# Block one keeps twenty tiles of its third convolution in place of sixteen and takes the statistics of twelve from a Gram matrix; the fused stage visits the tiles in a new order

## Chip, cores and metric

One core of one Trainium2 chip runs the whole program in one launch. The metric is the device time of that launch in microseconds (us). All data is float32. TensorE (PE) multiplies, VectorE (DVE), ScalarE (ACT) and GpSimd (POOL) do elementwise work, and DMAs are issued from the queues of SyncE (SP), ACT and POOL.

## The reference

Two residual bottleneck blocks run one after the other over 64 images of 1024 channels and 14x14 pixels. Batch norm uses the statistics of the whole batch, so each convolution must be known (or at least its mean and variance) for all images before any of its outputs can be scaled.

```python
def block(x, w1, b1, g1, be1, w2, b2, g2, be2, w3, b3, g3, be3, residual_scale):
    out = relu(_bn(_conv(x, w1, b1, 1, 0), g1, be1))      # 1x1, 1024 -> 256
    out = relu(_bn(_conv(out, w2, b2, 1, 1), g2, be2))    # 3x3, 256 -> 256
    out = _bn(_conv(out, w3, b3, 1, 0), g3, be3)          # 1x1, 256 -> 1024
    return relu(x + softplus(residual_scale)[0] * out)
x = block(x, ...)   # layer 0
x = block(x, ...)   # layer 1
```

## The kernel before

**Tiles and stages.** The batch is cut into T = 32 tiles of two images (392 pixels). A tile of x is 128 partitions by 8 rows (output-channel blocks `o`) by 392. The 256-channel output of conv 2 stays on chip for all tiles (`y_all`, 2 blocks). The stages are: conv 1 of block one; conv 2 of block one; `mixed`; `fused`; conv 2 of block two; `gram` of block two; `final`. The change touches `mixed` and `fused`.

**Seven products.** A 1x1 convolution of one unit is done as seven block products instead of eight (class `Seven`): `p1` to `p7`, with sums of the inputs made beforehand by elementwise engines. `Conv1` (block two's conv 1) has seven products of four matmuls each per tile, 28 in all; after `p1` it makes its input sums on DVE (`at3`, L439, then `at2`, L440, then `at1`, L441), `p6` needs `at2`, `p5` needs `at1`, and `p7`'s result is copied by ACT and added by DVE (L427). `Conv3` and `Direct` (conv 3) have seven products of one matmul each per unit, four units (`q`) per tile.

**Mixed.** Tiles are numbered so that 0 to KEPT-1 are the Gram tiles and KEPT to 31 the kept ones (KEPT = 16). Conv 3 of the kept tiles is computed here: tile KEPT whole in `first`, the other 15 as 60 `Direct` units. Their raw outputs z go to DRAM by DMA (`z<-kept`) and their statistics come from `bn_stats`. The Gram tiles' statistics come from the Gram matrix of their normed y: y is moved by DMA into `homes` (`move`, pieces `MOVES`), transposed by DVE (`turn`) in chunks of 128 pixels, and multiplied by `gram_products`, four small matmuls per chunk, in batches of BATCH = 4 chunks placed between units by the list `at`. 16 tiles are 6272 pixels, 49 chunks. `conv3_stats` turns the Gram matrix into mean and variance of conv 3 (no output of the Gram tiles is computed here), `bn_aggr` merges all entries (L1614), `affine` gives scale and shift. In the last units `bring` starts loading the first eight z rows (`at_first`).

**Fused.** The order of places is `positions()`: places 0, 2, 4 ... hold Gram tiles, places 1, 3, 5 ... kept ones. For each place x is loaded (`coming`, five buffers, the load for place p+4 at step 12 of place p, in four DMAs on SP), block one's third convolution is added, relu follows, the result is stored for block two's residual (`mid<-x`, ACT queue) and `Conv1` of block two reads it. For Gram places `last_convs` runs `Conv3` units: their matmuls are made here, DVE adds four parts (L514), POOL two, ACT does the relu. For kept places `kept_rows` takes the rows of z back from DRAM: an even row is one DVE operation (L1839), an odd row two POOL operations (L1825, L1826). A row's z lies in one of eight places in `y_all` that were loaded ahead (AHEAD = 8): the row eight further on is brought, by an SP DMA, when a row has been used (`behind`, `bring`). Only the last two tiles' rows use other places (28-element lines of `y_all`), and the last tile comes whole.

**The order.** One Python loop with a counter `k` writes the program, and each engine runs its part in that order. Step k gives one matmul of `Conv1` (28 steps per place). Beside it `done < LEAD + (k + 1) // 2` gives one `Conv3` matmul per two steps, and `k % 7 == 3` one kept row per seven steps. Before the loop, 14 `Conv3` matmuls (LAG) and seven rows are written. The rows of a step are written before its `Conv1` matmul, so they stand ahead of what that matmul's product asks of DVE.

Of the kernel before, what the change touches and what calls it, by code (L numbers as in the profile page):

```python
# [34 lines left out]

LAG, LEAD = 14, 10

KEPT = T // 2
NGRAM = KEPT * PX
MOVES = 5 * P * CH, 5 * P * CH, 5 * P * CH, 5 * P * CH, 9 * P  # L40
BATCH = 4
ROWS = 5 * CS, 13 * CS
AHEAD = 8


# [24 lines left out]
def bottlenecks(ctx: ExitStack, tc: tile.TileContext, x, w1s, w2s, w3s, pars, out):  # L70
# [1192 lines left out]
    def gram(psum, pool, homes, aff, minus_c, beside):  # L1263
# [142 lines left out]
                beside[k]()  # L1406
        return upper, lower, by, gs

    def positions():
        return [KEPT * (p % 2) + p // 2 for p in range(T)]  # L1410

    def beds(spare):


        places, before, last = [], {}, {}
        for r in range((T - KEPT - 1) * CS):
            t, o = KEPT + r // CS, r % CS
            if r < ROWS[1]:
                g, i = (NG - 3, NG - 1)[r >= ROWS[0]], r % AHEAD
                a = g * GPX + i % 4 * PX  # L1420
                key, v = (g, i), y_all[:, i // 4, a : a + PX]
            else:
                ring = [(u, s) for s in range(MS) for u in range(t, T)]
                i = o - MS
                key = ("spare", o % MS) if i < 0 or i >= len(ring) else ring[i]
                v = spare[key[1]] if key[0] == "spare" else two(*key)
            places.append(v)
            if key in last:
                before[r] = last[key]
# [15 lines left out]
    def mixed(psum, pool, one, x_right, x_left, aff, minus_c, w3, made_c, summed_c, summed_a, mv3, xs, coming_x):  # L1445
# [28 lines left out]

        def home(k):
            a, e = pieces[k]
            x = homes[k % 2][:, : MS * (e - a)].rearrange("p (s j f) -> p s j f", s=MS, j=4)
            return x, a, (e - a) // 4

        def quarter(k, i):  # L1480
            (a, e) = pieces[k]
            h = (e - a) // 4
            return slice(a + i * h, a + i * h + h)
# [8 lines left out]
        def move(k, i, places):  # L1492
            assert normed[k] >= MS * i + MS and (k < 2 or k - 2 in turned)
            for j in places:
                tc.keep_in_program_order(
                    nc.sync.dma_start(
                        out=home(k)[0][32 * i : 32 * i + 32, :, j], in_=y_all[32 * j : 32 * j + 32, :, quarter(k, i)]
                    )
                )
                moved[k] += 1  # L1500

        def blocks(t):
            return [[two(t, s)[:, i * H // 2 : (i + 1) * H // 2] for i in range(2)] for s in range(MS)]
# [63 lines left out]
        def chunks():  # L1567

            for k, (a, e) in enumerate(pieces):
                x, count = home(k)[0], (e - a) // P  # L1570
                for i in range(0, count, CH):
                    zt = next(zts)
                    turn(zt, x, i, min(CH, count - i))
                    if i + CH >= count:
                        assert moved[k] == 16
                        turned.add(k)
                    for c in range(min(CH, count - i)):
                        yield zt[:, c], (k, i + c)

        def batches():  # L1580
            queue, total = chunks(), NGRAM // P
            bounds = [*range(0, total, BATCH), total]
            ready = [[]]
            for _ in range(BATCH // CH):
                ready[0].extend(itertools.islice(queue, CH))
                yield
            for a, e in zip(bounds, bounds[1:]):
                for i, (v, _) in zip(range(a, e), ready.pop()):
                    gram_products(upper, lower, v, i == 0, i == total - 1, True)
                yield  # L1590
                ready.append([])
                for _ in range(BATCH // CH):
                    ready[0].extend(itertools.islice(queue, CH))
                    yield
# [2 lines left out]
        coming = {t: prepare(t) for t in range(KEPT + 1, T)}  # L1597
        tail, grams = None, iter(())
        moves = {}
        for k, begin in enumerate((3, 13, 20, 28), 1):  # L1600
            for i in range(8):
                moves[begin + i] = moves.get(begin + i, ()) + ((k, i // 2, (i % 2 * 2, i % 2 * 2 + 1)),)
        at = list(range(9, 48, 3))
        at_first, _ = beds((None, None))
        made = []

# [24 lines left out]
        for unit, step in stream:  # L1631
            t, q = KEPT + 1 + unit // 4, unit % 4
            if step == 1 and unit > 0:
                next(norms, None)
            if step == 3 and at[0] - 3 < unit < at[0]:
                grams = batches() if unit == at[0] - 2 else grams
                next(grams)
            if step == 2 and unit in at or step == 3 and (unit in at or unit - 1 in at):
                next(grams, None)
            if step == 3:  # L1640
                if q < 2 and t + 1 < T:
                    next(coming[t + 1], None)
                if 0 < unit <= 32 and unit % 2 == 0:
                    center((unit - 1) // 8 + 1, (unit - 1) % 8 // 2)
                for where in moves.get(unit, ()):
                    move(*where)
                if unit in (20, 23, 26, 29):
                    next(summed_a)
                if unit in (44, 48):
                    coming_x()  # L1650
                if 50 <= unit < 50 + AHEAD:
                    bring(at_first[unit - 50], unit - 50)
                if unit == 57:
                    assert next(tail, "end") == "end"
                    for half in range(2):
                        to = gram_entry[:, :, 3 * half : 3 * half + 3]
                        nc.gpsimd.memset(to[:, :, 0], NGRAM / 2)
                        run(nc.vector.tensor_copy(to[:, :, 1], mv3[:, :, 0]))
                        run(nc.vector.tensor_scalar(to[:, :, 2], mv3[:, :, 1], NGRAM / 2, None, ALU.mult))
            if step == 5 and q == 1 and t + 1 < T:  # L1660
                next(coming[t + 1], None)
            if step == 5 and unit == 57:
                column_sums(pool, blocks(positions()[2]), n, eng=nc.gpsimd, to=ahead())
            if unit == 59 and step in (3, 5):
                aggregated(step // 4)
            if step == 6 and unit > at[-1] + 1 and (tail is None or unit < 57):
                if tail is None:
                    assert next(grams, "end") == "end"
                    tail = conv3_stats(
                        psum, pool, (upper, lower, by, gs), w3, mv3, ("ax", "ap", "ax", "ap"), homes[1], ("ax", "ax", "ap")  # L1670
                    )
                next(tail, None)
# [116 lines left out]
    def fused(psum, pool, one, right, coming, xs, raw, w1, w3, aff, par, stats, border, begun):  # L1789
# [12 lines left out]
            behind[q].append(r)  # L1802

        def last_convs():
            for p in range(2, T, 2):
                t = places[p]
                ys = [[two(t, s)[:, i * H // 2 : (i + 1) * H // 2] for i in range(2)] for s in range(MS)]
                sums = column_sums(pool, ys, n, **(dict(to=ahead(), made=True) if p == 2 else {}))
                for q in range(CS // 2):
                    yield Conv3(psum, pool, xs[p], q, n, ys, sums, w3, aff, mids[t] if q == CS // 2 - 1 else None, one)  # L1810

# [4 lines left out]
        def kept_rows():  # L1816
# [10 lines left out]

            for o in 1, 3, 5:
                by_pool(*row(o, 1, o), o)
            for r, (p, o) in enumerate(itertools.product(range(1, T, 2), range(CS))):  # L1830
                while r == len(at) and later:
                    later.pop(0)()
                    yield
# [22 lines left out]

        whole = []
        pinned.append(True)
        a, c, rows = stream(first_convs(), T), stream(last_convs(), (KEPT - 1) * CS // 2), kept_rows()
        done, ended = LAG, None  # L1860
        for i in range(LAG):
            next(c)
            if i == 2:
# [4 lines left out]
        for k in itertools.count():  # L1868
# [7 lines left out]
                    nc.sync.dma_start(out=whole[0].rearrange("p s f -> p (s f)"), in_=zs[T - 1 - KEPT])  # L1876
                )
            late = k - 28 * (T - 4)
            if (late >= 30 and late % 5 == 0) if late >= 20 else k % 7 == 3:
                next(rows, None)  # L1880
            if next(a, "end") == "end":
                break
            while done < LEAD + (k + 1) // 2:
                if next(c, "end") == "end" and ended is None:
                    ended = k
                done += 1
            if ended is not None and k >= ended + 8:
                while waiting:
                    waiting.pop(0)()
        assert next(c, None) is None and next(rows, None) is None and not waiting  # L1890
# [322 lines left out]
```

## Time and profile before

| what | value |
|---|---|
| median of 3 runs | 1895.61 us (1895.54 to 1896.14) |
| profiled execution, its own time | 1896.71 us |
| span of its instructions | 1894.6 us |
| DVE, ACT, POOL busy in the span | 1574.0, 1092.0, 748.4 us |
| `mixed`, about | 586 to 787 us of the span |
| `fused`, about | 787 to 1235 us |
| mean DMA rate over the span | 242 GB/s |

Times inside the trace are microseconds from the span's start. A float32 matmul shows as two records, so counts of PE records are twice the matmuls of the program. A row of the timeline gives start, duration, engine, line, operation, output and input by name, and count of merged instructions; behind it, in brackets, stands how long the engine was idle before and what ended that. A few matmul records are missing from the trace.

### The profile page before, as it was taken

How to read it: one execution, taken by the hardware profiler on the slowest of the kernel's cores; microseconds unless marked ns; L12 is line 12 of the kernel's file. 1: busy time of each engine (PE TensorE's matmuls, PEld its weight loads, DVE VectorE, ACT ScalarE, POOL GpSimd, SP SyncE). 2: the span in 40 equal slices, each digit the busy share in tenths (PEclk: the TensorE clock that was granted, in tenths of full speed). 3: DMA queues.
4: the chain of work that ended last, by engine and by line, in shares of the span. 5: the costliest groups of instructions: out<-in, count | busy, mean ns of one | idle time of the engine just before them, and what ended most of it. 6: DMA issues, size and time to landing. Idle time of an engine off the chain costs nothing. (4 is left out here: it accounts for less than half of the span.)

```text
span 1894.6 us, 28577 instructions
## 1 busy us (share of the span) xinstructions
PE 1876.6 (99%) x9778; PEld 1563.6 (83%) x9778; DVE 1574.0 (83%) x2484; ACT 1092.0 (58%) x2275; POOL 748.4 (40%) x764
## 2 busy tenths in 40 slices
PE   9999999999999999999999999999999999999999
PEld 5555557999997998899999999999999986555555
DVE  5787867999998776778878788799999986888886
ACT  2222214677777665555555555457777692666666
POOL 0111100121206555377676776501121141666665
PEclk9999999999999999999999999999999999999999
DMA  7777654797764555678788889459788467799997
GB/s 288 271 252 258 223 184 131 206 217 219 206 201 161 181 177 204 248 272 308 279 278 309 281 302 285 193 168 223 212 208 226 141 160 289 262 346 345 334 354 270
DMA packets 262369, 458.19 MB, mean 242 GB/s; under 512 B 59152, under 2 KB 228976, under 8 KB 249040
## 3 DMA queue, kind: packets, MB, share of 16 engines
q1 hardware_dynamic: 224160, 373.28, 58.8%
q0 software_dynamic: 31216, 28.81, 7.8%
q10 hardware_dynamic: 6848, 54.28, 7.1%
q8 instruction: 78, 1.28, 0.3%
q14 instruction: 67, 0.55, 0.1%
HBM read 289.44 MB, written 141.03 MB: 227 GB/s over the span
## 5 line engine op out<-in xcount | busy, mean ns | idle before, releaser
L332 ACT ACTIVATE x<-x,shift 128x392 f32<-128x392 f32 x452 | 260.0, 614 | 77.2 <-DVE x L514 31.5
L159 PE MATMUL columns<-v,ub 128*128 128x224 f32 (+1 forms) x1536 | 302.5, 338 | 1.3 <-ACT columns L332 0.8
L159 PEld LDWEIGHTS columns<-v,ub 128*128 128x128 f32 x1536 | 268.8, 188 | 7.5 <-ACT columns L332 1.5
L332 ACT ACTIVATE cu<-cy,scale 128x196 f32<-128x196 f32 (+1 forms) x360 | 175.4, 499 | 166.5 <-PE cy L159 158.9
L159 PE MATMUL ay<-at,ws 128*128 128x196 f32 (+1 forms) x768 | 192.7, 382 | 1.4 <-DVE at L440 1.4
L159 PEld LDWEIGHTS ay<-at,ws 128*128 128x128 f32 x768 | 136.1, 190 | 36.5 <-issue 1.9
L514 DVE SCALAR_TENSOR_TENSOR x<-cp,scale,x 128x196 f32<-128x196 f32 (+1 forms) x240 | 124.6, 519 | 46.1 <-PE cp L159 44.7
L645 POOL TENSOR_TENSOR x<-x,cu 128x392 f32<-128x392 f32 x120 | 125.6, 1047 | 73.3 <-DVE x L514 72.1
L332 ACT ACTIVATE au<-ay 128x196 f32<-128x196 f32 (+1 forms) x140 | 53.8, 384 | 171.8 <-PE ay L159 157.8
L159 PE MATMUL l<-diffs,ub 128*128 128x224 f32 (+1 forms) x768 | 150.2, 338 | 0.3 <-ACT sd L1934 0.3
L159 PE MATMUL m<-sums,ua 128*128 128x224 f32 (+1 forms) x752 | 145.9, 336 | 0.0
L159 PEld LDWEIGHTS l<-diffs,ub 128*128 128x128 f32 x768 | 135.2, 190 | 1.3 <-ACT sd L1934 0.6
L159 PEld LDWEIGHTS m<-sums,ua 128*128 128x128 f32 x752 | 131.5, 189 | 0.8 <-DVE sums L761 0.2
L1059 POOL DMA_DIRECT2D y<-f x24 | 32.7, 1688 | 233.7 <-DVE f L979 233.7
L537 POOL TENSOR_TENSOR x<-x,cu 128x196 f32<-128x196 f32 (+1 forms) x120 | 105.1, 875 | 47.7 <-ACT cu L332 26.2
L159 PE MATMUL cx<-y,w 128*128 128x196 f32 (+1 forms) x396 | 122.2, 394 | 1.2 <-ACT cx L332 1.2
L159 PE MATMUL cy<-y,w 128*128 128x196 f32 (+1 forms) x372 | 117.0, 402 | 0.7 <-DVE y L1461 0.7
L542 POOL TENSOR_TENSOR x<-x,cu 128x392 f32<-128x392 f32 x60 | 79.2, 1320 | 84.9 <-DVE x L514 80.7
L332 ACT ACTIVATE y<-y,shift,scale 128x1568 f32<-128x1568 f32 (+7 forms) x94 | 106.7, 1153 | 7.8 <-DVE shift L1966 6.5
L206 POOL DMA_DIRECT2D u<-y x48 | 26.0, 543 | 212.4 <-ACT y L332 211.6
L940 ACT ACTIVATE columns<-m 128x448 f32<-128x448 f32 (+1 forms) x144 | 70.8, 492 | 58.8 <-PE m L159 54.0
L1825 POOL TENSOR_SCALAR y<-y,scale 128x392 f32<-128x392 f32 x57 | 92.4, 1622 | 28.8 <-DVE scale L2156 28.2
(303 smaller groups left out, 4556.6 us busy)
## 6 DMA issues: line engine op xcount, KB each, us to landing
ub<-u SPq DMA_DIRECT2D x92, 768.0 KB, 5.2
x<-in_x SPq DMA_DIRECT2D x35, 1568.0 KB, 8.0
mid<-x ACTq DMA_DIRECT2D x32, 1568.0 KB, 9.2
x<-mid SPq DMA_DIRECT2D x32, 1568.0 KB, 9.1
out<-x SPq DMA_DIRECT2D x123, 392.0 KB, 6.9
x<-in_x SPq DMA_DIRECT2D x108, 392.0 KB, 7.8
ua<-u SPq DMA_DIRECT2D x92, 256.0 KB, 3.0
z<-kept SPq DMA_DIRECT2D x60, 392.0 KB, 3.0
```

Source lines behind the costliest of these rows:

```text
L159: tc.keep_in_program_order(nc.tensor.matmul(*args, **kw))
L206: nc.gpsimd.dma_start(out=us[b][i][:, s, o], in_=u)
L332: tc.keep_in_program_order(nc.scalar.activation(*args, **kw))
L514: run(nc.vector.scalar_tensor_tensor(v, bank, self.scale[:, o : o + 1], v, ALU.mult, ALU.add))
L537: run(nc.gpsimd.tensor_add(self.part(1, 1), self.part(1, 1), u3))
L542: run(nc.gpsimd.tensor_add(v, v, self.u12))
L645: nc.gpsimd.tensor_add(v, v, self.u12[:, i * self.n : (i + 1) * self.n])
L940: copy(v, m, AF.Copy)
L1059: nc.gpsimd.dma_start(out=out_rows[3][:, o], in_=fa[:, o, :full], accum_op=ALU.add)
L1825: run(nc.gpsimd.tensor_scalar(z, z, scale[:, o : o + 1], None, ALU.mult))
```

## The change

KEPT becomes 12: tiles 0 to 11 are Gram tiles, 12 to 31 are kept. In `mixed` there are 76 `Direct` units in place of 60; the Gram matrix has 4704 pixels, 36.75 chunks, and the last piece is padded with zeros by POOL (`fill`) to make 37. Batches come every fifth unit in place of every third. Unit numbers that were written out (44, 48, 50, 57, 59) are counted from the end.

In `fused` the twelve Gram tiles stand at places 0, 2, 5, 8, 10, 13, 16, 18, 21, 24, 26 and 29 (`turns`). `Conv3` is a stream of its own for each Gram place, 28 matmuls and one empty step; `due(k)` lets the stream of place p run at one matmul per two steps from about k = 28(p-2) - 20 to 28(p-2) + 37, and none runs between two streams. Kept rows are written whenever `brought` is behind `LAG // 2 + (2 * k + 24) // 11`: two rows at k = 0, and then two per eleven steps. Loads of x stay at step 12 of each place.

```diff
-KEPT = T // 2
+KEPT = 12
 NGRAM = KEPT * PX
-MOVES = 5 * P * CH, 5 * P * CH, 5 * P * CH, 5 * P * CH, 9 * P
+MOVES = 5 * P * CH, 5 * P * CH, 5 * P * CH, NGRAM - 15 * P * CH
 BATCH = 4
-ROWS = 5 * CS, 13 * CS
+ROWS = 5 * CS, (T - KEPT - 3) * CS
...
+    def turns():
+
+        return [g * T // KEPT for g in range(KEPT)]
+
     def positions():
-        return [KEPT * (p % 2) + p // 2 for p in range(T)]
+        at = turns()
+        kept = iter(range(KEPT, T))
+        return [at.index(p) if p in at else next(kept) for p in range(T)]
...
-                g, i = (NG - 3, NG - 1)[r >= ROWS[0]], r % AHEAD
+                g, i = (KEPT // (GI // G) + 1, NG - 1)[r >= ROWS[0]], r % AHEAD
...
         def home(k):
             a, e = pieces[k]
-            x = homes[k % 2][:, : MS * (e - a)].rearrange("p (s j f) -> p s j f", s=MS, j=4)
+            run = -(-(e - a) // P) * 32
+            x = homes[k % 2][:, : MS * 4 * run].rearrange("p (s j f) -> p s j f", s=MS, j=4)
             return x, a, (e - a) // 4
+
+        def fill(k):
+
+            x, _, run = home(k)
+            if run % 32:
+                assert k - 2 in turned
+                nc.gpsimd.memset(x[:, :, :, run:], 0.0)
...
-            queue, total = chunks(), NGRAM // P
+            queue, total = chunks(), -(-NGRAM // P)
...
-        for k, begin in enumerate((3, 13, 20, 28), 1):
+        total = (T - KEPT - 1) * CS // 2
+        for k, begin in enumerate((3, 16, 27), 1):
...
-        at = list(range(9, 48, 3))
+        at = list(range(9, 55, 5))
...
         def last_convs():
-            for p in range(2, T, 2):
-                t = places[p]
+            for t, p in list(enumerate(turns()))[1:]:
+                yield from stream(units_of(t, p), CS // 2)
+                yield
+
+        def units_of(t, p):
+            for _ in range(1):
                 ys = [[two(t, s)[:, i * H // 2 : (i + 1) * H // 2] for i in range(2)] for s in range(MS)]
...
-            for r, (p, o) in enumerate(itertools.product(range(1, T, 2), range(CS))):
+            for r, (p, o) in enumerate(itertools.product([p for p in range(T) if places[p] >= KEPT], range(CS))):
...
-        a, c, rows = stream(first_convs(), T), stream(last_convs(), (KEPT - 1) * CS // 2), kept_rows()
-        done, ended = LAG, None
+        a, c, rows = stream(first_convs(), T), last_convs(), kept_rows()
+        done, ended, brought = LAG, None, LAG // 2
+
+        def due(k):
+
+            return max(29 * (g - 1) + min(29, LEAD + (k + 1 - 28 * (p - 2)) // 2) for g, p in enumerate(turns()) if g)
+
...
             late = k - 28 * (T - 4)
-            if (late >= 30 and late % 5 == 0) if late >= 20 else k % 7 == 3:
+            while brought < min(len(at) + 2, LAG // 2 + (2 * k + 24) // 11) and late < 20:
+                next(rows)
+                brought += 1
+            if late >= 30 and late % 5 == 0:
                 next(rows, None)
             if next(a, "end") == "end":
                 break
-            while done < LEAD + (k + 1) // 2:
-                if next(c, "end") == "end" and ended is None:
+            while done < due(k):
+                next(c)
+                done += 1
+                if done % 29 == 0:
                     ended = k
-                done += 1
-            if ended is not None and k >= ended + 8:
+            if done % 29 == 0 and k >= ended + 8:
```

More of the change, by code (lines that the diff above doesn't have):

```diff
@@ L1496, in move @@
                     nc.sync.dma_start(
-                        out=home(k)[0][32 * i : 32 * i + 32, :, j], in_=y_all[32 * j : 32 * j + 32, :, quarter(k, i)]
+                        out=home(k)[0][32 * i : 32 * i + 32, :, j, : home(k)[2]], in_=y_all[32 * j : 32 * j + 32, :, quarter(k, i)]
                     )
@@ L1569, in chunks @@
             for k, (a, e) in enumerate(pieces):
-                x, count = home(k)[0], (e - a) // P
+                x, count = home(k)[0], -(-(e - a) // P)
                 for i in range(0, count, CH):
@@ L1642, in mixed @@
                     next(coming[t + 1], None)
-                if 0 < unit <= 32 and unit % 2 == 0:
+                if 0 < unit <= 24 and unit % 2 == 0:
                     center((unit - 1) // 8 + 1, (unit - 1) % 8 // 2)
                 for where in moves.get(unit, ()):
+                    if where[1:] == (0, (0, 1)):
+                        fill(where[0])
                     move(*where)
@@ L1648, in mixed @@
                     next(summed_a)
-                if unit in (44, 48):
+                if unit in (total - 16, total - 12):
                     coming_x()
-                if 50 <= unit < 50 + AHEAD:
-                    bring(at_first[unit - 50], unit - 50)
-                if unit == 57:
+                if 0 <= unit - total + AHEAD + 2 < AHEAD:
+                    bring(at_first[unit - total + AHEAD + 2], unit - total + AHEAD + 2)
+                if unit == total - 3:
                     assert next(tail, "end") == "end"
@@ L1661, in mixed @@
                 next(coming[t + 1], None)
-            if step == 5 and unit == 57:
-                column_sums(pool, blocks(positions()[2]), n, eng=nc.gpsimd, to=ahead())
-            if unit == 59 and step in (3, 5):
+            if step == 5 and unit == total - 3:
+                column_sums(pool, blocks(1), n, eng=nc.gpsimd, to=ahead())
+            if unit == total - 1 and step in (3, 5):
                 aggregated(step // 4)
-            if step == 6 and unit > at[-1] + 1 and (tail is None or unit < 57):
+            if step == 6 and unit > at[-1] + 1 and (tail is None or unit < total - 3):
                 if tail is None:
@@ L1804, in last_convs @@
         def last_convs():
-            for p in range(2, T, 2):
-                t = places[p]
+            for t, p in list(enumerate(turns()))[1:]:
[3 more added lines that the diff above has]
+            for _ in range(1):
                 ys = [[two(t, s)[:, i * H // 2 : (i + 1) * H // 2] for i in range(2)] for s in range(MS)]
-                sums = column_sums(pool, ys, n, **(dict(to=ahead(), made=True) if p == 2 else {}))
+                sums = column_sums(pool, ys, n, **(dict(to=ahead(), made=True) if t == 1 else {}))
                 for q in range(CS // 2):
```

## The prediction

> **What bounds the kernel now.** I read the page first, then busy time by stage, then the timeline where the two changed stages begin and end.
>
> ```profile
> span 1894.6 us, 28577 instructions
> PE 1876.6 (99%) x9778; PEld 1563.6 (83%) x9778; DVE 1574.0 (83%) x2484; ACT 1092.0 (58%) x2275; POOL 748.4 (40%) x764
> ```
>
> TensorE is busy for 1876.6 of 1894.6 us, so a matmul that goes away is worth its time, and another engine counts only where it makes TensorE wait. The stages, with columns PE, weight loads, DVE, ACT, POOL, clock, DMA share, GB/s:
>
> ```profile
> 600.00:700.00 100.00, 98.51 (x731) 92.05 (x732) 79.22 (x187) 70.87 (x195) 60.18 (x71) 1.00 0.58 185
> 700.00:787.00 87.00, 86.26 (x556) 78.01 (x551) 59.90 (x145) 44.37 (x136) 35.78 (x43) 1.00 0.56 190
> 787.00:802.00 15.00, 13.66 (x56) 9.38 (x56) 13.04 (x35) 10.30 (x23) 9.16 (x9) 1.00 1.00 374
> 900.00:1000.00 100.00, 100.00 (x605) 99.62 (x603) 82.09 (x155) 57.04 (x131) 69.74 (x57) 1.00 0.80 285
> 1000.00:1100.00 100.00, 100.00 (x604) 99.66 (x604) 81.80 (x155) 56.63 (x128) 69.99 (x57) 1.00 0.81 286
> ```
>
> The mixed stage (600 to 787) leaves TensorE idle for 2.2 us, the middle of the fused stage for none. 605 records in 100 us are 0.33 us for a matmul of two records. DVE has 18% left in the fused stage, and between the two stages (787 to 802) the DMA engines are full, at 374 GB/s.
>
> **The change, part by part.**
>
> *Fewer Gram products.* One batch of four chunks in the mixed stage, on TensorE:
>
> ```profile
> 619.96 0.49 PE L159 MATMUL ay<-ct,wt 128*128 128x196 f32 x2
> 620.38 2.41 PE L159 MATMUL ap<-zt 128*64 128x193 f32 x32
> 622.73 0.60 PE L159 MATMUL ay<-ct,wt 128*128 128x196 f32 x2
> 623.16 0.49 PE L159 MATMUL cx<-y,w 128*128 128x196 f32 x2
> ```
>
> From the batch's start to the next matmul are 2.35 us; the steps into it (0.42) and behind it (0.43) are 0.09 and 0.10 over the usual 0.33. A batch costs 2.54 us. 49 chunks are twelve batches and a single chunk, 37 (36.75, filled up) are nine and a single one. Three batches go: -7.6 us. The zero fill is one small POOL operation, hidden where POOL has 40 of 100 us free.
>
> *Conv 3 of four tiles moves.* Sixteen units of seven products leave the fused stage and come to the mixed one: 112 matmuls, 37.0 us at 0.33, out of one and into the other. Net 0. Their ACT copies, DVE additions and statistics lie beside the matmuls (DVE 79.2, ACT 70.9 of 100). Without enough cover it costs what the mixed stage idles now, 2.2 us over 60 units, or 0.6 for 16; I take 0 and leave 0.6 to the range. The 16 more z stores queue on SP, which is not full there (DMA share 0.56).
>
> *Longer statistics.* An aggregation reads 21 entries in place of 17:
>
> ```profile
> L1614 DVE BATCH_NORM_AGGREGATE mv<-stats 128x2 f32<-128x102 f32 x7 | 3.7, 574 | 0.0
> ```
>
> 574 ns by 126/102 are 0.14 more; two stand between the last unit and the scale: +0.3 us.
>
> *Two rows at k = 0.* This is the wait that I think the change adds. The start of the fused stage now:
>
> ```profile
> 786.67 3.47 SPq L109 DMA_DIRECT2D x<-in_x  x3
> 794.85 17.10 SPq L1443 DMA_DIRECT2D y<-z  x11
> 800.65 0.96 DVE L439 TENSOR_TENSOR at<-x 128x784 f32<-128x784 f32 x1
> 800.68 1.49 PE L159 MATMUL ay<-x,w 128*128 128x196 f32 x8
> 801.64 0.97 DVE L440 TENSOR_TENSOR at<-at,x 128x784 f32<-128x784 f32 x1
> 803.33 0.89 PE L159 MATMUL ay<-at,ws 128*128 128x196 f32 x4
> 807.29 0.63 DVE L1839 SCALAR_TENSOR_TENSOR x<-y,scale,x 128x392 f32<-128x392 f32 x1 [2.72 <-DMA y<-z]
> ```
>
> SP issues three whole loads of x, then, from 794.85, the z rows that take the places of used ones. Row 8 (first of place 3) uses the place of row 0, so its transfer is the first of these and queues behind 4.8 MB of x. DVE waits for it until 807.29. Today that costs TensorE nothing: row 8 is written at k = 10, behind the sums of the first Conv1 tile. After the change rows 7 and 8 are written at k = 0, so row 8 stands on DVE ahead of L439. Behind it wait the three sums, and the additions that free the bank of conv 3; `p6` (803.33 now) needs L440's result, and every later matmul stands behind `p6`. Nothing ahead of that transfer changes, so it lands by 807.29; then 0.63 for the row, 0.96 and 0.97 for the sums and 0.14 to the matmul give 809.99. Late by 6.7 us. Bounds: 0, if the row's transfer is there in time, and 6.7; I take 6.7, since the queue ahead of it is the same.
>
> A wait of that length also cost clock elsewhere. Where the fused stage ends:
>
> ```profile
> 1236.00:1240.00 4.00, 2.06 (x8) 1.26 (x7) 3.70 (x14) 1.38 (x5) 0.14 (x2) 0.91 0.76 250
> 1240.00:1244.00 4.00, 4.00 (x16) 3.73 (x15) 3.83 (x9) 2.34 (x5) 0.00 (x0) 0.67 0.63 217
> 1238.71 1.75 PE L159 MATMUL columns<-sums,ua 128*128 128x224 f32 x5 [1.94 <-DVE sums L761]
> ```
>
> After a wait of 1.94 us the granted clock is 0.91 and 0.67 over two stretches of 4 us: 0.36 + 1.32, or 1.7 us of work lost. The 6.7 us wait should bring the same: +1.7 (0 to 1.7).
>
> *Conv1 alone.* Gram places now lie two or three apart, seven times three. A stream takes 58 steps, so in 84 steps some 26 have no Conv3 matmul between Conv1's; before, one in three was Conv3's until the last tiles. From `p7`'s end to the next `p6` lie 19 matmuls with a stream (6.3 us) and 12 without (4.0 us). In that time ACT copies, DVE adds (L427) and makes L439 and L440. Alone it occurs at the end of the fused stage:
>
> ```profile
> 1210.47 1.49 PE L159 MATMUL ay<-at,ws 128*128 128x196 f32 x8
> 1211.80 1.49 PE L159 MATMUL ay<-x,w 128*128 128x196 f32 x8
> 1212.83 0.33 ACT L332 ACTIVATE au<-ay 128x196 f32<-128x196 f32 x1 [0.40 <-PE ay L159]
> 1213.53 0.63 DVE L1839 SCALAR_TENSOR_TENSOR x<-whole,scale,x 128x392 f32<-128x392 f32 x1
> 1214.09 1.27 DVE L439 TENSOR_TENSOR at<-x 128x784 f32<-128x784 f32 x1
> 1215.40 1.75 DVE L440 TENSOR_TENSOR at<-at,x 128x784 f32<-128x784 f32 x1
> 1217.29 1.56 PE L159 MATMUL ay<-at,ws 128*128 128x196 f32 x8 [1.16 <-DVE at L440]
> 1221.35 1.49 PE L159 MATMUL ay<-at,ws 128*128 128x196 f32 x8
> 1225.70 4.22 PE L159 MATMUL ay<-at,ws 128*128 128x196 f32 x24 [0.21 <-DVE at L440]
> ```
>
> `p7` begins at 1210.47 and ends by 1211.80, and `p6` comes at 1217.29, having waited 1.16 us, with a row's 0.63 on DVE between. The next pass (1222.68, which is 1221.35 and four matmuls, to 1225.70) had no row and took 3.02, under 4.0. In the built order eight more passes have the short way; two of them carry a row ahead of L440. Bounds: 0 (3.02 is under 4.0) and 8 x 1.16 = 9.3. POOL works through rows in these stretches as it did at 1214, so I go by that pass: two at 1.16, six at 1.16 - 0.63 = 0.53. Sum +5.5.
>
> *Loads close to their first use.* x of place p is loaded at step 28(p-4) + 12; row r of the kept tiles is written when 2k + 24 reaches 11(r-6). Before, 26 steps lay between. Now at places 19, 27 and 30 (first rows 88, 128, 144) it is 439 - 432 = 7, 659 - 656 = 3 and 747 - 740 = 7 steps, 1.5 matmuls each, or 3.5, 1.5 and 3.5 us.
>
> ```profile
> DMA to landing us min/median/max: 3.1/7.8/11.1
> mid<-x ACTq DMA_DIRECT2D x28, 1568.0 KB, 9.3
> x<-in_x SPq DMA_DIRECT2D x108, 392.0 KB, 7.8
> y<-z SPq DMA_DIRECT2D x95, 196.0 KB, 5.8
> ```
>
> The first line is for the parts of x. A row's first use needs only the first of the four parts, which is nearest to the least, 3.1 us: DVE then waits 1.6 at place 27 and not at the others. TensorE's slack is 6.3 less the 5.49 of the slow pass (1211.80 to 1217.29), 0.8, which leaves +0.8. Bounds 0, and with the median landing (6.3 - 0.8) + 2 x (4.3 - 0.8) = 12.5.
>
> *Sum:* -7.6 + 0.3 + 6.7 + 1.7 + 5.5 + 0.8 = +7.4. The profiled execution took 1896.7 us (span 1894.6 and 2.1 around it), 1.1 over the median. 1904.1 on its scale, 1903.0 beside the median 1895.6.
>
> **The rivals.**
>
> *A: row 8's transfer comes in time.* Place: the first DVE row of place 3. It decides whether the transfer lands before 800.65. For it: a z row alone takes about 5.8. Against it: it starts at 794.85 behind three x loads, and the DMA engines are full. Without the 6.7 and 1.7 the sum is -1.0: 1894.6, not slower.
>
> *B: the Conv1 passes are hidden.* The pass without a row had 1.0 us to spare (4.0 - 3.02). Then 5.5 falls away: 1897.5, within what can be told from no change. With A as well, only matmuls count: 1896.7 - 7.6 + 0.3 + 0.8 - 1.1 = 1889.1, faster.
>
> *C: the DMA engines become the bound in the fused stage.* In 28 steps alone (9.3 us) a load, a store and 5.1 rows are due, 1568 + 1568 + 1000 KB, or 4.23 MB: 455 GB/s. At 374, the rate of the full stretch, that takes 11.3 us; seven such stretches fall behind by 2.0 each, 14.0, in place of the 5.5 and 0.8: -7.6 + 0.3 + 8.4 + 14.0 = +15.1, 1910.7. Against it: with a stream beside it (13.9 us for 28 steps) the same bytes need 305 GB/s, so five buffers can catch up in the 58 steps.
>
> The Trainium skill (DMA: Bandwidth & Descriptors, Where 436 GB/s comes from) gives two ceilings: 435 GB/s for the ports between the DMA engines and on-chip memory, and about 358 for one core's share of the memory behind them. By the first each stretch falls behind by only 0.4 us and rival C ends near 1899.7, by the second by 2.5 and near 1914.3, both estimates. The full stretch of this trace, 374 at a share of 1.00, lies above the second and far below the first, and C goes by it.
>
> **How the numbers follow.** A measurement of this kernel tells a change from none at about 0.2%, 3.8 us: same is 1891.8 to 1899.4. Forecast (1903.0): 0.55. C: 0.12. B: 0.16. A: 0.10. A with B: 0.07. Slower 0.67, same 0.26, faster 0.07. The terms at their lowest give 1888.3 (only -7.6 and 0.3), at their highest 1896.7 - 7.6 + 0.9 + 8.4 + 9.3 + 12.5 - 1.1 = 1919.1. For 8 in 10 I leave out A with B below and the top end of the late loads above: 1893 to 1911.
>
> **What would show it.** Right: TensorE waits some 6 us for L440 just after the fused stage begins, with DVE waiting for `y<-z` before it, and a granted clock under 1 there; nine waits of 0.3 to 1.2 us for L440 some 37 us apart; Gram records down by 96, mixed stage longer by 29 to 30 us. Wrong: no such wait at the start (A), a dense fused stage (B), DMA share near 1 through it with waits for x (C).

## The result and the profile after

The changed kernel takes 1956.86 us (median of 5 runs, 1955.07 to 1959.05) beside 1895.78 (5 runs, 1895.54 to 1897.09): 1.0322 times as long, interval 1.0307 to 1.0337. It is slower, as forecast, but by 61 us, not by 7; 1956.9 lies outside the range of 1893 to 1911. The profiled execution took 1955.07 us.

The page's first lines:

```profile
span 1953.3 us, 28576 instructions
PE 1888.3 (97%) x9682; PEld 1572.0 (80%) x9682; DVE 1580.6 (81%) x2470; ACT 1095.7 (56%) x2299; POOL 792.5 (41%) x797
```

The 96 records less are the three Gram batches. The span grew by 58.7 us: TensorE's idle time from 18.0 to 65.0 (+47.0), its busy time by 11.7, although 7.6 us of work went. The stages (columns as in the prediction):

```profile
700.00:816.00 116.00, 115.21 (x723) 107.16 (x722) 80.03 (x198) 66.12 (x202) 59.66 (x72) 1.00 0.53 185
836.60:843.40 6.80, 4.07 (x13) 4.10 (x14) 6.13 (x9) 0.95 (x2) 6.44 (x4) 0.50 1.01 395
830.00:1262.00 432.00, 384.01 (x2186) 374.90 (x2186) 315.26 (x542) 212.30 (x476) 300.96 (x232) 0.96 0.79 280
```

Mixed is as dense as before. All the loss is in the fused stage: 48 us idle, and a mean clock of 0.96 over 432 us. The second row is one of eight stretches at half clock, each at or just behind the end of a long wait, 34.1 us together. TensorE is busy in only 28.3 of them (4.07 of 6.80 in this row), because five of them begin while it still waits, so they cost half of that, some 14 us of work. Where the expectations below take half of a whole stretch of 6.8 us, that is more than 1 us too much. The DMA engines are busy 0.79 of the time. At the start:

```profile
826.06 16.43 SPq L1449 DMA_DIRECT2D y<-z  x9
830.37 0.83 PE L159 MATMUL ay<-x,w 128*128 128x196 f32 x4
836.48 0.62 DVE L1860 SCALAR_TENSOR_TENSOR x<-y,scale,x 128x392 f32<-128x392 f32 x1 [6.06 <-DMA y<-z]
837.02 0.97 DVE L439 TENSOR_TENSOR at<-x 128x784 f32<-128x784 f32 x1
838.02 1.16 DVE L440 TENSOR_TENSOR at<-at,x 128x784 f32<-128x784 f32 x1
839.33 0.99 PE L159 MATMUL ay<-at,ws 128*128 128x196 f32 x2 [6.14 <-DVE at L440]
```

The stage begins at 830.37, 29.7 us later than before (800.68): the predicted 29 to 30. Then the predicted wait: DVE stands at row 8 until its z has landed, the sums follow, TensorE has lost 6.14 us. But that is one wait of many. Who waits for what from 816 to 1300 (total, times, longest):

```profile
PE ay L159 <- ACT au L332: 15.6, 4, 5.9
PE cp L159 <- DVE x L514: 11.7, 13, 3.1
PE cy L159 <- DVE ct L478: 10.6, 6, 6.7
PE ay L159 <- DVE at L440: 9.3, 6, 6.1
```

```profile
ACT au L332 <- DMA y<-z: 10.1, 2, 5.1
ACT y L332 <- DMA mid<-x: 8.5, 1, 8.5
ACT x L332 <- DMA w<-z: 7.2, 1, 7.2
ACT x L332 <- DMA x<-in_x: 5.1, 1, 5.1
...
DVE x L1860 <- DMA x<-in_x: 16.0, 3, 5.5
```

With a wait of 2.9 us for `y<-z` at the stage's start, ACT waits 33.8 us for transfers (the expectations below count the four rows, 30.9). Among them are `y<-z` and `w<-z`, which the waiting instructions do not read. One such place, in the timeline:

```profile
902.13 0.33 ACTq L554 DMA_DIRECT2D mid<-x  x1
913.21 0.33 ACTq L1876 DMA_DIRECT2D mid<-x  x1
913.59 0.42 ACT L332 ACTIVATE y<-ay,par 128x196 f32<-128x196 f32 x1 [8.46 <-DMA mid<-x]
914.04 0.57 DVE L430 BATCH_NORM_STATS2 stats<-y 128x6 f32<-128x392 f32 x1 [6.64 <-ACT y L332]
916.88 0.99 PE L159 MATMUL cy<-ct,wt 128*128 128x196 f32 x2 [6.66 <-DVE ct L478]
```

The stores of a Conv3 tile (902.13) and of a kept tile (913.21) now come close together. In the built order each transfer on SP's and ACT's queues waits for the landing of the one eight before it in the program: the trace shows them taking eight semaphores in turn, and POOL's transfers eight others. Seven transfers of SP lie between the two stores, so the eighth before the second store is the first one. The second therefore stands on ACT until the first has landed, 11 us after its issue (the row's `mid<-x`); behind it wait Conv1's copy, DVE, the column sums and TensorE, 6.66 us. Loads are late too:

```profile
944.22 7.10 SPq L1449 DMA_DIRECT2D y<-z  x3
951.42 3.94 SPq L109 DMA_DIRECT2D x<-in_x  x4
958.83 0.63 DVE L1860 SCALAR_TENSOR_TENSOR x<-y,scale,x 128x392 f32<-128x392 f32 x1 [5.53 <-DMA x<-in_x]
```

SP takes its transfers in order. Three transfers of z rows take SP from 944.22 to 951.3, 5.9 us of it a wait for POOL to free the place of the third; the load of x stands behind them and DVE waits 5.53 us for it.

### The profile page after: what moved, and what is told of

Same layout as the page of the kernel before. It is cut to its first block, busy times and chain, and to the rows that moved or that the text cites. A ratio compares the mean times of both kernels' runs of the same rounds, so it can differ in the third digit from the quotient of the medians.

```text
span 1953.3 us, 28576 instructions
## 1 busy us (share of the span) xinstructions
PE 1888.3 (97%) x9682; PEld 1572.0 (80%) x9682; DVE 1580.6 (81%) x2470; ACT 1095.7 (56%) x2299; POOL 792.5 (41%) x797
## 5 line engine op out<-in xcount | busy, mean ns | idle before, releaser
L332 ACT ACTIVATE cu<-cy,scale 128x392 f32<-128x392 f32 (+1 forms) x312 | 158.2, 513 | 151.0 <-PE cy L159 147.1
L645 POOL TENSOR_TENSOR x<-x,cu 128x392 f32<-128x392 f32 x120 | 125.6, 1048 | 73.1 <-DVE x L514 72.2
L514 DVE SCALAR_TENSOR_TENSOR x<-cp,scale,x 128x392 f32<-128x392 f32 (+1 forms) x208 | 111.0, 534 | 42.3 <-PE cp L159 38.8
L1846 POOL TENSOR_SCALAR y<-y,scale 128x392 f32<-128x392 f32 x73 | 126.3, 1729 | 25.8 <-DVE scale L2186 23.3
L537 POOL TENSOR_TENSOR x<-x,cu 128x392 f32<-128x392 f32 (+1 forms) x104 | 95.5, 918 | 99.0 <-ACT cu L332 56.7
L605 DVE BATCH_NORM_STATS2 stats<-kept 128x6 f32<-128x392 f32 x152 | 85.4, 562 | 55.0 <-ACT kept L332 54.1
L332 ACT ACTIVATE y<-y,shift,scale 128x1568 f32<-128x1568 f32 (+7 forms) x86 | 101.0, 1195 | 7.8 <-DVE shift L1996 6.5
L159 PE MATMUL ay<-at,w 128*128 128x196 f32 (+1 forms) x376 | 95.6, 389 | 10.0 <-ACT au L332 10.0
```

Source lines behind the costliest of these rows:

```text
L159: tc.keep_in_program_order(nc.tensor.matmul(*args, **kw))
L332: tc.keep_in_program_order(nc.scalar.activation(*args, **kw))
L514: run(nc.vector.scalar_tensor_tensor(v, bank, self.scale[:, o : o + 1], v, ALU.mult, ALU.add))
L537: run(nc.gpsimd.tensor_add(self.part(1, 1), self.part(1, 1), u3))
L605: run(nc.vector.bn_stats(self.stats[:, self.o[row], self.t - KEPT, :], self.z[:, row]))
L645: nc.gpsimd.tensor_add(v, v, self.u12[:, i * self.n : (i + 1) * self.n])
```

## The experiments

Medians; the kernel before, run beside them, stood at 1895.3 to 1896.3, and intervals are of the ratio to it. Unless said otherwise the edit is made to the changed kernel.

**One suspect each.**

e1, both stores of the fused stage on SP (the one at L1876 is shown; the one at L554 is changed in the same way):

```diff
-                nc.scalar.dma_start(out=mids[places[p]], in_=xs[p].rearrange("p s f -> p (s f)"))
+                tc.keep_in_program_order(
+                    nc.sync.dma_start(out=mids[places[p]], in_=xs[p].rearrange("p s f -> p (s f)"))
+                )
```

> The stores of finished tiles (`mid<-x`) are issued from SP's queue in place of ACT's; nothing else. Theory S (a store that stands in ACT's order waits for older transfers, and everything behind it on ACT waits with it): ACT's five waits for transfers (10.1 + 8.5 + 7.2 + 5.1 = 30.9 us in the changed kernel's trace) go, TensorE's waits for `au` (15.6) and the long one for `ct` (6.7) go with them, and about half of the 34 us at half clock: 1957 - 22 - 8 = some 1927. Rival L (the rows stand too close behind the transfers that feed them): the wait only moves to SP, loads and z rows start later, 1950 to 1975. Rival U (uneven streams of Conv3 alone): unchanged, 1953 to 1960.

1935.8 (1.0196 to 1.0230), -21.1. ACT no longer waits for a transfer, and TensorE's waits for `au` are gone; the loads stay late (DVE 22.6 us for `x<-in_x`, 16.0 before the edit). Theory S holds for two thirds of what it promised.

e2, a later start of the rows:

```diff
-            while brought < min(len(at) + 2, LAG // 2 + (2 * k + 24) // 11) and late < 20:
+            while brought < min(len(at) + 2, LAG // 2 + min((2 * k + 24) // 11, k // 5)) and late < 20:
```

> Rows are written one per five steps until that catches up with two per eleven (near k = 120); later rows stand where they were. Row 8 stands at k = 10 as in the kernel before. The prediction's own step (row 8 waits on DVE ahead of the sums for `p6`): TensorE's wait of 6.1 us at 839 goes and 6.8 us at half clock with it, 1957 - 6.1 - 3.4 = 1947.5. Rival: the start only moves the wait, the next row or load waits instead: 1954 to 1960.

1946.1 (1.0251 to 1.0281), -10.8: the prediction's wait, with its clock. By the trace these are 6.1 and 2.1 us; each run's interval is nearly 3 us wide to either side.

e3, `column_sums` of the next tile called at the end of a stream:

```diff
+            after = None
             for t, p in list(enumerate(turns()))[1:]:
-                yield from stream(units_of(t, p), CS // 2)
+                ys, sums = after or sums_of(t)
+                yield from stream(units_of(t, p, ys, sums), CS // 2)
+                after = sums_of(t + 1) if t + 1 < KEPT else None
                 yield
```

> The four column sums of the next Gram tile are written at the end of a Conv3 stream, some 26 steps before they are used, not at the start of the next stream. Theory S and L: only the five short waits of TensorE for `ct` go (10.6 less the one of 6.7 us, which ACT's wait made): -3.9 us, 1953. Rival U (the restart of a stream is a main cost): the waits for `cp` and `cy` behind a restart go too, -10 us or more, under 1947.

1957.3 (1.0308 to 1.0339), no gain, which neither theory had. The waits for `ct` went, those for `cp` rose from 11.7 to 20.5: with loads and stores late, DVE's time is not what decides.

e4, each z row brought two rows later:

```diff
-                for q in behind[r]:
+                for q in behind[r - 2]:
```

> The transfer of a z row is written two rows later than the row whose place it takes, so SP waits less for POOL and DVE (142.9 and 26.1 us in the trace) ahead of the loads of x. Theory L in the form that SP's order holds the loads back: DVE's three waits for `x<-in_x` (16.0 us) and the one of ACT (5.1) go, TensorE wins 2.5 + 4.1 + 3.1 + 0.8 = 10.5 us and about 5 of clock: 1941. Rival: z rows now come late in place of the loads, with new waits for `y<-z`: 1957 or more. Theory S alone: the loads gain, the waits of ACT for its stores stay: 1945 to 1955.

1930.3 (1.0168 to 1.0198), -26.6. In e4 some rows of the last tiles use their place before it is filled, so its outputs are wrong; f1 mends that.

**The causes together.** f1 is e4's edit for the rows of the eight places alone (`q < ROWS[1]`); f2 adds e2, f3 adds e3 to f2, f4 adds e1 to f2.

> A z row's transfer is written two rows later, as in e4_bring_two_later, but only for the rows that go round the eight places; the rows of the last tiles, which use other places, are brought where the changed kernel brings them. Theory L (SP's order: a bring that waits for POOL or DVE holds back the loads behind it, and ACT's stores wait for the transfers so delayed): e4's gain of 26.6 us stays, and its one long wait near 1195 (10.9 us of DVE for `y<-z`, 6.9 of TensorE, 6.8 us at half clock), which came from the rows of the last tiles, goes: 1930 - 6.9 - 3.4 = 1920. Rival: that wait was not from the late bring of the last tiles' rows: 1930.

> f1_bring_later together with the later start of the rows of e2_row8_later. If the two causes are separate the gains add: f1's time - 10.8, some 1909. Rival: the wait for row 8 also gave the transfers behind it time, so the gain is smaller: f1's time - 5 or less.

> f2_bring_row8 and the column sums of the next Gram tile written at the end of a stream. In e4 nine waits for `ct` (8.2 us) and the waits for `cp` that follow 25 us behind them are what is left of short waits. If the sums at the restart make them: f2's time - 8, some 1901. Rival, as e3 alone showed (no gain, waits for `cp` grew from 11.7 to 20.5): the work only moves on DVE, f2's time within 2.

> f2_bring_row8 and the stores of finished tiles from SP's queue. Theory L: with SP's order freed, ACT waits for transfers only 6.2 us (e4), none of it seen by TensorE, so the stores' queue no longer matters: f2's time within 3. Rival S (ACT's order is a cause of its own): f2's time - 8 or more.

f1: 1926.5 (1.0145 to 1.0175), -30.4 in all, between its two expectations: DVE's wait near 1195 went, and a wait of ACT for `w<-z` took its place. Waits of f1 for transfers, and SP's:

```profile
ACT x L332 <- DMA w<-z: 7.0, 1, 7.0
ACT x L332 <- DMA y<-z: 3.4, 2, 2.9
ACT au L332 <- DMA x<-in_x: 2.1, 1, 2.1
...
DVE x L1860 <- DMA x<-in_x: 4.1, 1, 4.1
...
SPq L1449 <- POOL x L1847: 130.9, 44, 8.1
SPq L109 <- PE ap L159: 22.9, 5, 7.4
SPq L109 <- DMA mid<-x: 14.7, 6, 3.4
```

Against the changed kernel, whose SP has these:

```profile
SPq L1449 <- POOL x L1847: 142.9, 42, 8.1
SPq L109 <- DMA y<-z: 9.6, 8, 2.4
SPq L109 <- PE ap L159: 8.8, 1, 8.8
```

SP waits for POOL nearly as long as before, so e4's expectation was wrong in its means. What changed is where the loads (L109) stand: they come early, and wait for their own buffer, until the matmuls that read it are done (22.9) or its store has landed (part of the 14.7). Their waits for older transfers of z halve, 9.6 to 4.9. Counted against the Conv1 matmul of the step at which each load is written, SP issues the 27 loads of the stage 0.8 us behind it on average in the changed kernel, and 2.3 us ahead of it in f1. ACT's 33.8 us became 12.5, DVE's 16.0 became 4.1.

f2: 1919.8 (1.0109 to 1.0139), f1 - 6.7, between the two expectations. f3: 1909.8 (1.0053 to 1.0087), f2 - 10.0: the sums at a restart cost 10 us once loads and stores are in time, which e3 alone could not show. f4: 1917.2 (1.0096 to 1.0126), f2 - 2.6: with SP's order right, ACT's stores hardly matter.

**Controls, and the ring.** b1 is f1's edit and b2 the prediction's step alone, both in the kernel before; h1 loads x in one transfer (`coming(1)` for `coming(4)`); g1 is f3 with the last tiles' first rows brought one by one.

> Control: the kernel before with z rows brought two rows later, as f1_bring_later has it. Its TensorE has no wait in the middle of the fused stage, so if the edit is worth time only where a store or a load is late, nothing changes: 1894 to 1897. Rival (the edit is a gain of its own): 1892 or less.

> Control: the kernel before with rows 7 and 8 written at k = 0 (not at 3 and 10), all other rows where they were: the prediction's step alone. By the prediction +6.7 for the wait and +1.7 for the clock: 1904. By e2_row8_later, which took it away from the changed kernel: +10.8, 1906. Rival A (row 8's transfer is in time, or the wait is made up later): 1895 to 1898.

> The changed kernel with x of a place loaded by one transfer in place of four; the bytes are the same. In the built order each transfer of SP's and ACT's queues waits for the landing of the one eight before it in the program. If that ring is what a store on ACT waits for (theory ring), fewer transfers between a store and its eighth before make that one older, ACT's 30.9 us of waits for transfers fall under 10 and TensorE's `au` and long `ct` waits (22 us) go, less what the first rows lose that now wait for a whole load: 1930 to 1945. Rival (only SP's order counts, the number of transfers does not): ACT's waits stay, DVE's waits for `x<-in_x` (16.0) grow: 1957 to 1975.

> f3_bring_row8_sums, and the first rows of the last tiles are brought one by one as their places come free (five of eight, 3 to 8 rows earlier) in place of all eight behind row 135. What is left long in f3 is one wait: ACT waits 7.1 us for `w<-z` (a transfer of the last tiles' rows, that a store stands behind), TensorE 5.9 for `au`, with 6.8 us at half clock behind. Theory L: spread out, these transfers land before the store asks: 1909.8 - 5.9 - 3.4 = 1900.5. Rival: the queue of transfers there is full anyway, the wait moves to the next load: 1907 to 1912.

b1: 1896.1 (0.9992 to 1.0011), no change: the edit wins only where something is late. b2: 1905.3 (1.0034 to 1.0064), +9.5, and its rows are the predicted ones:

```profile
PE ay L159 <- DVE at L440: 8.2, 3, 6.9
...
DVE x L1839 <- DMA y<-z: 7.0, 1, 7.0
```

h1: 1970.5 (1.0377 to 1.0408), slower by 13.7, yet its rows split the two costs:

```profile
ACT x L332 <- DMA y<-z: 2.8, 1, 2.8
...
DVE x L1860 <- DMA x<-in_x: 44.8, 6, 11.4
```

With fewer transfers in the ring ACT's waits fall from 33.8 to 2.8 us, as only the ring predicts; and the first rows now wait for whole loads, 44.8 us. The total came out as the rival had it, for a cause that both had.

g1: 1911.2 (1.0068 to 1.0098), no better than f3; the wait of ACT for `w<-z` (7.0) stayed.

**What is left.** s2 and g2 put both stores on POOL's queue (`nc.gpsimd.dma_start`), in the changed kernel and in f3; g3 is f2 with the stores on POOL and one Conv3 stream for all tiles (`stream(last_convs(), (KEPT - 1) * CS // 2)`, sums made with a tile's first unit); g5 is f3 with one more tile in the eight places (`ROWS = 5 * CS, (T - KEPT - 2) * CS`), and with the first rows of the rest brought one by one, as in g1.

> The changed kernel with the stores of finished tiles issued from POOL's queue, which has transfers of its own and does not stand in the ring of eight of SP and ACT; rows and loads as in the changed kernel. Theory ring: ACT's 30.9 us of waits for transfers go as in e1_store_sp, and SP, which keeps neither ACT's waits nor 32 of its transfers in the ring, is at least as early as there: 1936 or less, with DVE's waits for `x<-in_x` under 22.6. Rival: what e1 won came only from a later store, and POOL, in order behind its rows, stores so late that the next loads wait: 1945 to 1960.

> f3_bring_row8_sums with the stores from POOL's queue. Left in f3: one wait of ACT for `w<-z` ahead of a store (TensorE 5.9 for `au`, 3.4 of clock), 6.0 for `cp` at the ends of the streams, 2.4 for L440. Theory ring: the first goes, the others stay: 1909.8 - 9.3 = 1900.5. Rival (as f4 and g1: the place is late whatever queue stores, DVE or ACT wait for the load there): 1907 to 1917.

> g2_store_pool with the units of all Gram tiles in one Conv3 stream, as the kernel before has it (it pauses after the first matmuls of the next unit, so no stream ends or starts between tiles), at the same steps. If the ends of the streams make the 6.0 us of waits for `cp` and the sums at the start those for `ct`, both are gone: g2's time - 5, near 1895.5 and so no slower than the kernel before. Rival (the bank waits come from the pace beside Conv1, not from the ends): g2's time within 2, or a bit slower as the sums are written late again.

> f3_bring_row8_sums with the rows of one more tile in the eight places: ten of the transfers of the last two tiles' rows, in lines of 28 elements (SP stands about 4 us at some of them in g1's trace: 1167.23 to 1171.28), become four, and they come one place later. If those transfers are what the store near 1177 stands behind, ACT's wait of 7 us, TensorE's of 5.9 and 3.4 of clock go: 1909.8 - 9.3 = 1900.5. Rival (the order of loads, stores and rows is too tight there whatever the rows' places): the wait moves, 1906 to 1913. In neither case is it under the kernel before: 6.0 of waits for `cp` and 2.4 for L440 stay.

s2: 1939.3 (1.0215 to 1.0246), -17.5, between its expectations and near e1: either queue frees ACT. g2: 1912.2 (1.0071 to 1.0101), not the gain expected; DVE waits for a load at the same place instead. g3: 1918.3 (1.0102 to 1.0135), 6 us slower than g2, which neither expectation had. It has no wait for `ct`, and no stream ends between tiles, yet this row is larger than f3's 6.0:

```profile
PE cp L159 <- DVE x L514: 14.5, 16, 5.2
```

One of the waits is a late load (5.2); the others come as often as before, so the ends of the streams do not make them. g5: 1904.0 (1.0030 to 1.0057), f3 - 5.8. Transfers of the kind of which g5 has four in place of ten, as SP issues them in g1:

```profile
1166.06 5.12 SPq L1449 DMA_DIRECT2D y<-z  x3
1171.28 2.99 SPq L1449 DMA_DIRECT2D w<-z  x2
1174.38 1.79 SPq L109 DMA_DIRECT2D x<-in_x  x4
```

Three transfers in lines of 28 elements (the first row) hold SP for 5.1 us, and a load behind them. The first `w<-z` behind them, a whole row, holds it for 2.5 as well, so it is not shown that the short lines alone do it. g5's fused stage:

```profile
830.00:1204.00 374.00, 364.70 (x2160) 356.91 (x2159) 317.66 (x532) 210.74 (x470) 305.24 (x229) 1.00 0.88 320
```

```profile
PE cp L159 <- DVE x L514: 5.4, 11, 0.8
PE ay L159 <- DVE at L440: 2.2, 5, 0.6
```

The clock is full and no wait of TensorE is over 0.9 us. At 605 records in 100 us (the prediction's row of the kernel before) 2160 take 357 us, so some 17 of the 374 are short waits, part of which is counted as busy. Some 5 of them lie in the seven stretches between two Conv3 streams, 74.1 us in all, in which 417 records begin (68.9 us at that rate). The other 12 lie beside the streams.

**The short waits.** g7 and g8 allow a row only at six steps of a place (`step in (1, 14, 17, 20, 23, 26)`, and `(3, 7, 10, 17, 21, 24)`), in g5.

> g5_ring_longer with each row written at one of the steps 1, 14, 17, 20, 23, 26 of a place (rows up to 12 steps later), so that none stands on DVE between the sums of Conv1 (step 4) and the adds that free Conv3's bank near step 12. g5 has about 16 us of short waits in the fused stage (the kernel before has 1), for `cp` and L440 most of them. Theory D (a row in that stretch of DVE's order makes them, the prediction's term for Conv1's short passes, with the place of the row deciding): -6 to -10, 1894 to 1898, no slower than the kernel before. Rival (DVE and POOL are behind whatever the order, since 152 rows come in the time of 104): 1902 to 1908, the waits only change places.

> g5_ring_longer with each row written at one of the steps 3, 7, 10, 17, 21, 24 of a place; 3, 10, 17 and 24 are the steps of the kernel before, where TensorE did not wait. Theory D: the rows at 7 and 10 stand in the critical stretch, so the waits stay: 1902 to 1906, 4 or more above g7. Rival: any even grid helps, within 2 of g7.

g7: 1920.4 (1.0112 to 1.0146), 16 us slower; g8: 1903.1 (1.0024 to 1.0051), like g5. Rows of g7:

```profile
PE cp L159 <- DVE x L514: 9.7, 17, 1.1
PE ay L159 <- DVE at L440: 5.7, 7, 1.1
...
ACT x L332 <- DMA mid<-x: 8.1, 1, 8.1
```

Theory D falls: with rows away from the sums both kinds of short wait grew (from 6.3 and 2.7 in g5 over the same part of the trace), and one store met the ring again, which with its clock is about half of the 16 us. g8 is not above g7, as theory D had it, but 17 us below. Its waits for `cp` are 2.5 us and those for L440 4.6, at nearly the total of g5: there the waits changed places, as g7's rival had it. No version beats the kernel before; g8 and g5 come nearest, 7 to 8 us over it. What the short waits beside the streams are made of was not separated.

## Why the prediction was right and wrong

- **Fewer Gram products, conv 3 moved:** right. 96 records less, mixed longer by 29.7 us and dense.
- **Two rows at k = 0:** right in place, order and size: 6.14 us for 6.7. Its **clock drop** came near too: 1.7 was forecast, and 6.8 us at half clock, with TensorE busy in 4.1 of them, are 2.1. That is in part luck, as the 1.7 was read off a stretch behind a much shorter wait. With both, 10.8 (e2) and 9.5 (b2) for 8.4. Rival A falls.
- **Conv1 alone:** the waits for L440 came shorter and fewer than forecast (9.3 - 6.1 = 3.2 us in five, for 5.5 in eight), but visible waits are not all. In g5, where little else is late, the stretches without Conv3 take some 5 us too long, so the size was about right and rival B falls. What the sum lacked are the 12 us of short waits beside the streams; those for Conv3's bank (`cp`, 5.4) are part of them, the rest stays open.
- **Loads close to their first use** is the step that failed. It put the load's landing at 3.1 us behind the step where it is written, "DVE then waits 1.6 at place 27 and not at the others", +0.8. The load does not start where it is written: SP takes it in order, behind z rows that wait for their places, and in the ring of eight. DVE waited 16.0 us in three waits, at places 11, 27 and 30. There SP issued the load 3.6, 3.4 and 3.1 us behind the Conv1 matmul of its step, and its first part landed 7.3, 4.4 and 4.7 us after that; in f1 SP issued the first two 3.2 us ahead of the matmul. ACT waited 33.8, which no term had, because a store in ACT's order stands in the same ring. f1 took 30.4 us away without touching a row or a load's place in the step count.
- **Left out:** the four sums at each restart of a Conv3 stream, 10.0 us (f3 - f2), and the slow transfers of the last tiles' rows, 5.8 (g5 - f3; the other part of g5's edit, alone in g1, won nothing).
- **Rival C** foresaw loads too late in the fused stage, but from full DMA engines. Their share is 0.79 at 280 GB/s, and g5 moves 320 at 0.88 with DVE's waits for loads at 4.9 us in place of 16.0: what made them late was mainly order. C was right about the place: in g5's seven stretches without Conv3 the share is 0.91 to 1.02, at 314 to 406 GB/s, yet no load there costs TensorE more than 0.9 us. The Trainium skill (DMA: Bandwidth & Descriptors, Where 436 GB/s comes from) has ceilings of 358 and 435; the stretch of 395 at 836.6 lies above the first, as the 374 of the prediction did.
- **The sum:** of the 61 us, e2 took away 10.8, f1 30.4, and f2, which has both, 37.0 (they overlap by 4.2); the sums 10.0, the last rows 5.8. That leaves g5 8.4 over the kernel before, which is -7.6 for the Gram batches and 16.0 of other loss: near the 17 of short waits worked out from its records.

## What to carry to other kernels

When work that is fed by transfers is packed closer, cost the queues, not the landing times: for each load, list what stands ahead of it in its queue's order and what that waits for, and for each store, what stands behind it on its engine. A transfer written where its place becomes free holds back all later ones; written two rows later it cost nothing where nothing was late (b1). Price a wait of TensorE with the clock that it loses, but only for the time that TensorE is busy again.

## What was not expected of the hardware

The half clock comes in steps. Waits of 6.1 to 6.7 us came with 6.8 us at half clock (the row 836.60 to 843.40), and the 1.94 of the prediction with about 3.4. Length alone does not decide: in the changed kernel a wait of 5.92 us came with 3.4, and one of 1.95 (the same wait as the prediction's, now at 1299.26) with none. The eight stretches begin at 836.6, 867.4, 915.1, 959.5, 1031.2, 1102.9, 1188.2 and 1222.3, which lie whole multiples of 3.413 us apart, so where a wait falls between such marks may decide; no run moved a wait to test it. The Trainium skill (TensorE: Matmul & The Clock Gate, What's actually happening) says that the clock halves after at least one idle window of about 3.4 us and comes back after a busy one of that length. The lengths agree; the drop after 1.94 us of idleness is shorter than the page's window.

DVE's sums take longer beside some of POOL's operations. L440 in the middle of the fused stage, in the kernel before:

```profile
L440 DVE TENSOR_TENSOR at<-at,x 128x784 f32<-128x784 f32 x29 | 35.9, 1236 | 1.0
```

and in g5:

```profile
L440 DVE TENSOR_TENSOR at<-at,x 128x784 f32<-128x784 f32 x29 | 43.0, 1484 | 1.0
```

The mean of 1484 ns hides two kinds. In the kernel before, 28 of the 29 take 1243 to 1249 ns. In g5, 11 take 1162 to 1249, 17 take 1669 to 1746, and one 975. One of each kind, with what POOL does beside it; the first two rows are of the kernel before, the others of g5:

```profile
813.34 1.24 DVE L440 TENSOR_TENSOR at<-at,x 128x784 f32<-128x784 f32 x1
812.45 1.98 POOL L1825 TENSOR_SCALAR y<-y,scale 128x392 f32<-128x392 f32 x1
```

```profile
881.01 1.67 DVE L440 TENSOR_TENSOR at<-at,x 128x784 f32<-128x784 f32 x1
880.11 1.75 POOL L1852 TENSOR_TENSOR x<-x,y 128x392 f32<-128x392 f32 x1
```

In all 17 long ones an addition of POOL (L542 or L1852) runs beside L440 for some 0.8 us or more; in the 11 shorter ones it is a row's first operation, as in the kernel before. The one of 975 runs beside a shorter addition (L537), so not every addition does it. Where POOL stood still, at 1133.51 in g8, L440 took 0.97 us. L440 alone takes 7 us more of DVE in g5 (43.0 for 35.9), with other operations of POOL beside it; how much of it TensorE feels was not separated. The Trainium skill (SBUF — State Buffer, SBUF: two separate sides) says that a DVE operation with two on-chip inputs and a POOL operation that reads on-chip memory exclude each other; the rows agree in direction.
